# A block of attention and spectral filtering: projection loads in smaller parts, some of its products ahead of time, and the second norm taken from the spectrum

## The chip, the cores and the metric

One core of a Trainium2 chip runs the whole program. The metric is the device time of one execution in microseconds (us); the kernel before took 3833.35 us (median of three runs, 3829.59 to 3835.82). A profiled execution beside them gives the trace that is quoted below. Its engines are TensorE (PE; its weight loads are listed apart as PEld), VectorE (DVE), ScalarE (ACT), GpSimd (POOL) and SyncE (SP), which issues all DMA transfers of this kernel.

## What is computed

The input x has 2 images of 48 x 48 tokens with 768 channels, all in float32. Cut to what matters:

```python
x = x + attention(group_norm(x))     # 12 heads of 64, relative positions, a projection 768 x 768
x = x + spectral(group_norm(x))

def spectral(x):                     # x: 2, 48, 48, 768
    xf = rfft2(x, axes=(1, 2), norm="ortho")         # 48 x 25 frequencies
    o1 = gelu(block_matmul(xf, w1) + b1)             # 8 blocks of 96 channels, complex
    o2 = softshrink(block_matmul(o1, w2) + b2, 0.01) # 8 blocks of 96 channels, complex
    return irfft2(o2, s=(48, 48), norm="ortho")

def group_norm(v):                   # 32 groups of 24 channels, over all tokens of an image
    return (v - mean(v)) / sqrt(var(v) + 1e-5)
```

The second norm has no scale of its own, so it commutes with the Fourier transform: the mean sits in one coefficient of each channel, the one of frequency zero, and the division by the deviation is a factor on each channel. By Parseval's theorem the sum of squares over the tokens is also the sum of squares over the spectrum.

## The kernel before

The two images run one after the other. Each passes through four stages.

**Attention.** After the first norm, 108 units (6 pairs of heads, 6 groups of 384 queries, 3 thirds of a group) run through a loop whose order is written out by hand: operations recorded through `InOrder` (L59, all of them shown as L67 in the profile) keep the program's order on their engine. For a unit, PE computes the scores (`ps_s`), DVE adds the relative positions that POOL has laid out (L342) and takes the maximum, ACT takes the exponential, DVE transposes squares of 32, and SP moves the pieces to their place in `pT`, six DMAs per half of a unit. Two turns later `weigh` multiplies `pT` by the values into `ps_o`, and `finish` stores the result, group by group, in the DRAM tensor `oT`; the softmax denominators go to `inv_d`, inverted, for half of a pair's groups at a time. In the last turns of the loop, L555 calls `late()` seven times; each call runs one step of the class `Projection` (L572), beside the attention's own work.

**Projection.** `Projection` owns one large SBUF tile: the weights `w` (6 blocks of 128 rows by 768), the bias `pb`, two buffers for `oT` and one for the inverses. Its seven steps (L586) load the weights in two halves, then nothing, then `tokens(0)`, nothing, the bias, and `values_bias`, which for the first image adds the values' bias multiplied by the projection's weights (`ps_pb`, 12 matmuls). `tokens(g)` (L625) loads 384 columns of `oT` in one DMA and the inverses in two, and POOL multiplies them (L639). `project_out` (L643) loads the residual x in six parts of 4 x 96 rows at its start, adds the bias on POOL (L657), and then runs over 18 tiles of 128 tokens. For each tile and each half of the channels PE makes a product `acc` of six matmuls (L693), and DVE adds it into x in pieces whose rows stay inside one of the 96-row parts (`shifts`, L702). Behind the products, `over_w` (L665) transforms two image rows at a time along w: four matmuls `ps_y`, four ACT copies, and one DMA to the DRAM tensor `y_d`. `tile_stats` (L723) takes the sum and the squared deviations of each 96-row part on DVE, POOL and ACT for the second norm; `join_stats` (L736) joins them after the last tile, with two matmuls `js_tot` and a square root on ACT.

**Spectrum.** `Spectral.run` (L998) goes over 8 blocks of 96 channels, two of which make a slab. `load` reads a slab's `y_d` into five `y2` tiles (L867). `over_h` (L870) transforms along h: 25 small matmuls in five groups `ps_z`, which DVE and ACT in turn copy to the one buffer `z`. `scale` multiplies the weights w1 by the deviation's inverse, and `constant` subtracts the mean from the frequency zero. `first` (L893) is the product with w1, 24 records of 400 columns for PE and a GELU on ACT; `second` (L914) is the product with w2, where DVE adds the bias (L939) and clips (L945) and POOL subtracts (L946). In `run`, block n goes through `over_h(n)`, `second(n-1)`, `first(n)`, in this order on PE. `back_h` and `back_w` return to image rows, through the DRAM tensor `u_d`, and write `out`.

What is not recorded through `InOrder` is placed by a scheduler when the program is built: in this kernel the products, the x loads and additions, the stats and most of the spectrum. All of it shares one pool of seven PSUM banks (`ps_b`); `ps_o` has a bank to itself.

Of the kernel before, what the change touches and what calls it, by code (L numbers as in the profile page):

```python
# [9 lines left out]
F32 = mybir.dt.float32  # L10
AF = mybir.ActivationFunctionType
ALU = mybir.AluOpType
# [4 lines left out]
P = 128  # L17
# [144 lines left out]
def attention(tc, k, x_b, a, oT, inv_d, late, span, ps_b, ps_o):  # L162

# [10 lines left out]
    with ExitStack() as ctx:  # L174
# [319 lines left out]
        for n in range(len(order) + 3):  # L494
# [33 lines left out]
            if turn is not None:  # L528
                turn()
                turn = None  # L530
            if n > 1 and recent:
                older = recent.pop(0)
                weigh(older)
# [38 lines left out]
class Projection:  # L572


    def __init__(self, tc, k, a, oT, inv_d, span, ps_b, dram):
# [7 lines left out]
        self.o = {}  # L583
        w_v = a["proj_w"].rearrange("(cc p) f -> p cc f", p=P)
        half = NCC // 2
        self.steps = [  # L586
            lambda: nc.sync.dma_start(out=self.w[:, :half], in_=w_v[:, :half]),
            lambda: nc.sync.dma_start(out=self.w[:, half:], in_=w_v[:, half:]),
            lambda: None,
            lambda: self.tokens(0),  # L590
            lambda: None,
            self.bias,
            self.values_bias,
        ]

    def step(self):
        self.steps.pop(0)()

# [5 lines left out]
    def values_bias(self):  # L604


        nc, k = self.nc, self.k
        if k.pb_d is not None:
            return
        for hf in range(2):  # L610
            cols = slice(hf * UQ, (hf + 1) * UQ)
            ps = self.ps_b.tile([P, 512], F32, tag="b", name="ps_pb")
            for cc in range(NCC):
                nc.tensor.matmul(
                    ps[:, :UQ],
                    lhsT=k.bv[:, cc : cc + 1].to_broadcast([P, P]),
                    rhs=self.w[:, cc, cols],
                    start=(cc == 0),
                    stop=(cc == NCC - 1),
                )  # L620
            nc.vector.tensor_tensor(self.pb[:, cols], ps[:, :UQ], self.pb[:, cols], ALU.add)
        k.pb_d = self.dram.tile([C], F32, tag="pb_d", name="pb_d")
        nc.sync.dma_start(out=k.pb_d, in_=self.pb[0, :])

    def tokens(self, g):  # L625

        nc = self.nc
# [5 lines left out]
        nc.sync.dma_start(out=o_sb, in_=self.oT_v[:, :, g * UQ : (g + 1) * UQ])  # L633
        for h in range(2):
            nc.sync.dma_start(
# [3 lines left out]
        nc.gpsimd.tensor_tensor(o_sb, o_sb, inv, ALU.mult)  # L639
        self.o[g] = o_sb  # L640


def project_out(tc, k, x_b, pr, pools, y_d, x2, stats, constants):  # L643
# [6 lines left out]
    ps_b, small, work = pools  # L650
# [3 lines left out]
    for i, part in enumerate(x2):  # L654
        nc.sync.dma_start(out=part, in_=x_v[:, i * XP : (i + 1) * XP, :])
        for j in range(XP):
            nc.gpsimd.tensor_tensor(part[:, j, :], part[:, j, :], pr.pb[:R], ALU.add)  # L657
        if i == 0:
            constants()
            pr.tokens(1)  # L660
    row = lambda hp: x2[hp // XP][:, hp % XP, :]
    local = small.tile([R, HW // 2, NG], F32, tag="local", name="local")
    dev = small.tile([R, HW // 2, NG], F32, tag="dev", name="dev")

    def over_w(g):  # L665
# [4 lines left out]
        for s in range(C // SC):  # L670
# [10 lines left out]
        nc.sync.dma_start(out=y_d[:, 2 * g : 2 * g + 2, :], in_=y1)  # L681

    done = turned = 0
    for t in range(NT):
        if t % 3 == 0:
            if t // 3 not in pr.o:
                pr.tokens(t // 3)
            o_sb = pr.o[t // 3]
        for hf in range(2):
            cols = slice(hf * UQ, (hf + 1) * UQ)  # L690
            acc = bank("acc")
            for cc in range(NCC):
                nc.tensor.matmul(  # L693
                    acc[:, :UQ],
                    lhsT=o_sb[:, cc, (t % 3) * P : (t % 3 + 1) * P],
                    rhs=pr.w[:, cc, cols],
                    start=(cc == 0),
                    stop=(cc == NCC - 1),
                )
# [3 lines left out]
        while (turned + 1) * 2 * R <= (t - 1) * P:  # L703
            over_w(turned)
            turned += 1
        while (done + 1) * R <= (t + 1) * P:
            tile_stats(
                nc,
                lambda name: work.tile([R, C], F32, tag="st", name=name),
                row(done),  # L710
                local[:, done, :],
                dev[:, done, :],
            )
            done += 1
    while turned < HW // 4:
        over_w(turned)
        turned += 1
    mean, rstd = join_stats(nc, k, small, bank, local, dev)
    nc.vector.tensor_copy(stats[:, 0, :], mean)
    nc.vector.tensor_copy(stats[:, 1, :], rstd)  # L720


def tile_stats(nc, work, xt, local, dev):  # L723

    x3 = xt.rearrange("p (g d) -> p g d", d=GC)
    nc.vector.tensor_reduce(local, x3, AX.X, ALU.add)
    nc.vector.tensor_scalar(local, local, 1.0 / GC, None, ALU.mult)  # L727
    xc = work("st_xc").rearrange("p (g d) -> p g d", d=GC)
    nc.gpsimd.tensor_tensor(  # L729
        xc, x3, local[:, :, None].to_broadcast([xt.shape[0], NG, GC]), ALU.subtract  # L730
    )
    nc.scalar.activation(xc, xc, AF.Square)  # L732
# [447 lines left out]
```

## Time and profile before

| what | us |
|---|---|
| median of three runs | 3833.35 |
| the profiled execution's own time | 3833.92 |
| its span, first to last instruction | 3831.8 |
| image 0: first product to last ps_y on PE | 1471.29 to 1660.7 |
| image 0: spectrum, first ps_z to last ps_x | 1672.05 to 1912.8 |
| image 1: first product to last ps_y on PE | 3382.52 to 3572.1 |
| image 1: first ps_z | 3583.56 |
| L693 products, PE busy, both images | 293.7 |
| L729 POOL / L732 ACT, busy, both images | 70.9 / 40.5 |

The mean clock granted to PE over the span is 0.978 of full speed. A row of the page's fifth part gives the line, engine, operation, output and input tile with their shapes, the count, then the busy time and the mean of one in ns, and then how long the engine was idle just before and who ended that. Matmuls in float32 appear as two records each, so the 12 matmuls of one tile's products are 24 records. The timeline lists the same instructions in order of time, neighbours of a kind merged. A row of the windows gives, for a stretch of time, the busy time of PE, PEld, DVE, ACT and POOL, the clock granted to PE, and the busy share and rate of the DMA engines.

### The profile page before, as it was taken

The page shows a single profiled execution, that of the slowest core. Times are in us where ns is not written, and L with a number is a line of the kernel's source. Part 1 is how long each engine was busy: PE and PEld are TensorE (multiplying, and loading weights), DVE is VectorE, ACT ScalarE, POOL GpSimd, SP SyncE. Part 2 cuts the span into 40 slices and gives each one's busy share as a digit, 9 for nine tenths or more (in the row PEclk, how much of TensorE's full clock was granted, in tenths as well). Part 3 has the DMA queues.
Part 4 walks back from the last instruction along what each step waited for, and adds up shares of the span by engine and source line. Part 5 has one row for each costly group of instructions (what it writes and reads, how often), then busy time and mean ns, then how long its engine had stood idle before and what let it go on. Part 6 is the DMA issues. An engine that isn't in the chain of part 4 may idle for free.

```text
span 3831.8 us, 83222 instructions
## 1 busy us (share of the span) xinstructions
PE 3657.1 (95%) x31464; PEld 2591.2 (68%) x31464; DVE 2940.4 (77%) x6642; ACT 2501.8 (65%) x3550; POOL 2063.8 (54%) x646
## 2 busy tenths in 40 slices
PE   8999999999999888989989999999999999779899
PEld 6677777767777655566666767777677776555665
DVE  5788888989889884654557988988888889846544
ACT  3788888888888882222137888888888888822221
POOL 2566666666666666422125666666666666663121
PEclk9999999999999999999999999999999999989899
DMA  3677777777777888434526787777777777884344
GB/s 109 144 175 170 169 175 167 177 160 175 169 171 170 172 194 199 128 85 125 175 74 143 171 176 169 172 171 173 167 175 167 173 169 164 203 192 124 88 122 134
DMA packets 496092, 606.92 MB, mean 158 GB/s; under 512 B 180109, under 2 KB 310797, under 8 KB 495694
## 3 DMA queue, kind: packets, MB, share of 16 engines
q1 hardware_dynamic: 495694, 601.61, 67.3%
q8 instruction: 250, 4.10, 0.5%
q14 instruction: 148, 1.21, 0.1%
HBM read 131.53 MB, written 87.67 MB: 57 GB/s over the span
## 4 chain that ended last, share of the span: by engine, by line
PE 80%; DMA 7%; DVE 4%; POOL 4%; SPq 3%; issue 1%; ACT 1%; POOLq 0%; DVEq 0%
PE ps_o L67 20%; PE ps_s L67 19%; PE ps_proj L67 14%; PE ps_v L67 8%; PE acc L693 5%; PE ps L929 4%; DVE s L67 3%; POOL s L342 3%; DMA pT<-s 3%; SPq L67 2%; PE ps_z L877 2%; PE ps_u L960 2%; PE ps L902 2%; PE ps L906 2%; PE ps_r L67 2%; DMA x<-in_x 1%
## 5 line engine op out<-in xcount | busy, mean ns | idle before, releaser
L342 POOL TENSOR_TENSOR s<-rhw 128x2304 f32<-128x2304 f32 x432 | 1744.7, 4060 | 1144.6 <-DMA pT<-s 596.9
L67 DVE CUSTOM_DVE_ANT_0 s<-ps_s,s 128x512 f32<-128x512 f32 (+1 forms) x2160 | 1224.0, 633 | 373.7 <-issue 248.3
L67 ACT ACTIVATE s<-s,nm 128x1152 f32<-128x1152 f32 x864 | 1074.7, 1245 | 451.7 <-DVE nm L67 414.1
L67 DVE STREAM_TRANSPOSE s<-s 128x1152 f32<-128x1152 f32 x864 | 1111.8, 1344 | 5.5 <-ACT s L67 5.5
L67 ACT COPY pT<-s 32x1152 f32<-32x1152 f32 x864 | 993.3, 1150 | 24.6 <-PE ps_o L67 9.2
L67 PE MATMUL ps_o<-pT,v 128*64 128x128 f32 x15552 | 923.9, 279 | 75.2 <-DMA pT<-s 47.4
L67 PEld LDWEIGHTS ps_o<-pT,v 128*64 128x64 f32 x15552 | 872.2, 140 | 138.2 <-issue 61.6
L67 PE MATMUL ps_s<-kT,qT 64*128 64x512 f32 (+1 forms) x4320 | 919.5, 558 | 13.8 <-DVE mx L67 9.9
L67 PEld LDWEIGHTS ps_s<-kT,qT 64*128 64x128 f32 x4320 | 431.0, 186 | 452.3 <-issue 334.8
L67 PE MATMUL ps_proj<-xnT,w 128*128 128x384 f32 (+1 forms) x2016 | 597.3, 450 | 2.3 <-ACT gn_rstd L150 2.3
L67 PEld LDWEIGHTS ps_proj<-xnT,w 128*128 128x128 f32 x2016 | 360.5, 191 | 209.6 <-DVE mx L67 41.1
L693 PE MATMUL acc<-proj 128*128 128x384 f32 x864 | 293.7, 500 | 21.4 <-DVE x L702 11.9
L67 PEld LDWEIGHTS ps_v<-w,xnT 128*128 128x128 f32 x2592 | 295.8, 193 | 21.2 <-DVE mx L67 21.2
L67 PE MATMUL ps_v<-w,xnT 128*128 128x128 f32 x2592 | 308.0, 278 | 0.0
L946 POOL TENSOR_TENSOR spectrum<-spectrum 128x480 f32<-128x480 f32 x80 | 96.3, 1203 | 324.9 <-DVE spectrum L945 322.0
L693 PEld LDWEIGHTS acc<-proj 128*128 128x128 f32 x864 | 168.9, 196 | 142.6 <-issue 22.9
L732 ACT ACTIVATE st_xc<-st_xc 96x768 f32<-96x768 f32 x48 | 40.5, 843 | 233.8 <-POOL st_xc L729 233.8
L67 DVE DVE_READ_ACCUMULATOR2_ANT mx<- 128x1 f32 x2160 | 179.8, 83 | 0.0
L702 DVE TENSOR_TENSOR x<-acc,x 32x384 f32<-32x384 f32 (+2 forms) x216 | 119.6, 554 | 78.4 <-PE acc L693 74.4
L67 ACT ACTIVATION_READ_ACCUMULATOR s<-s,nm 128x1 f32 x864 | 161.1, 186 | 0.0
L729 POOL TENSOR_TENSOR st_xc<-x,local 96x768 f32<-96x768 f32 x48 | 70.9, 1481 | 145.6 <-DVE local L727 129.0
L910 ACT ACTIVATE spectrum<-ps,b 96x400 f32<-96x400 f32 x96 | 56.6, 590 | 138.7 <-PE ps L906 138.7
(96 smaller groups left out, 2194.7 us busy)
## 6 DMA issues: line engine op xcount, KB each, us to landing
pT<-s SPq DMA_DIRECT2D x2592, 144.0 KB
t<-rel SPq DMA_DIRECT2D x144, 189.0 KB
rhw<-t SPq DMA_DIRECT2D x144, 144.0 KB
y_d<-y SPq DMA_DIRECT2D x24, 672.0 KB
y<-y_d SPq DMA_DIRECT2D x40, 360.0 KB
u_d<-spectrum SPq DMA_DIRECT2D x40, 360.0 KB
u<-u_d SPq DMA_DIRECT2D x48, 300.0 KB
xt<-in_x SPq DMA_DIRECT2D x12, 1152.0 KB
```

Of the source, the lines that this page charges most:

```text
L67: return lambda *args, **kw: self.tc.keep_in_program_order(op(*args, **kw))
L342: nc.gpsimd.tensor_tensor(s[:, h, :].rearrange("p (y x) -> p y x", x=HW), rhw[:, x, h, :HW][:, :, None].to_broadcast([P, HW, HW]), rhw[:, ...
L693: nc.tensor.matmul(acc[:, :UQ], lhsT=o_sb[:, cc, (t % 3) * P : (t % 3 + 1) * P], rhs=pr.w[:, cc, cols], start=(cc == 0), stop=(cc == NCC - 1),
L702: nc.vector.tensor_tensor(dst, acc[p : p + n, :UQ], dst, ALU.add)
L729: nc.gpsimd.tensor_tensor(xc, x3, local[:, :, None].to_broadcast([xt.shape[0], NG, GC]), ALU.subtract)
L877: nc.tensor.matmul(ps[:BS, w * 96 : (w + 1) * 96], lhsT=self.y2[s, j][:, w, i * BS : (i + 1) * BS], rhs=k.fh, start=True, stop=True,)
L902: nc.tensor.matmul(ps[:BS, :400], lhsT=w1[:, wa, i, :], rhs=zf[:, 0, fs], start=True, stop=False,)
L906: nc.tensor.matmul(ps[:BS, :400], lhsT=w1[:, wb, i, :], rhs=zf[:, 1, fs], start=False, stop=True,)
L910: nc.scalar.activation(self.o1[:, ri, fs], ps[:BS, :400], AF.Gelu, bias=self.b1[:, n, ri : ri + 1])
L929: nc.tensor.matmul(ps[64 * r : 64 * r + 64, w * BS : (w + 1) * BS], lhsT=self.o1[:, ri, f0 : f0 + 64], rhs=w2[:, (0, 2, 1, 0)[2 * r + ri], ...
L946: nc.gpsimd.tensor_tensor(val, val, clip, ALU.subtract)
L960: nc.tensor.matmul(ps[: 2 * HW, :480], lhsT=k.ih, rhs=d2[:, c0 : c0 + 480], start=True, stop=True)
```

## The change

The change has four parts.

1. `tile_stats`, `join_stats`, `norm`, `scale` and `constant` go. In `Spectral`, each block's squares are summed on ACT as soon as its groups are in `z` (`square`: twice for the frequencies that stand for two, once for the first and last column), `mean(n)` subtracts the group's mean from the frequency zero after a matmul with the constant matrix `gmean` (one column, `ps_nm`), and `norm(n)` joins the sums over a group with a second such matmul (`ps_nv`), takes the inverse square root on DVE by a shift of the bits and three Newton steps, and scales block n's part of w1.
2. `z` has two buffers, and `over_h(n+1)` runs ahead of `second(n-1)` and `first(n)`. The mean and the norm of block n+1 stand inside `second(n-1)`, after its first and fourth group.
3. `Projection` loads its weights in six parts over three turns, `oT` in two halves, and issues its loads, multiplications and products in program order (`InOrder`, so these show as L68). `tokens(1)` is a step of its own in the last turns. `fill` puts matmuls between the last three `weigh` calls: for image 0 one half of `values_bias`, then the other and one product, then three products; for image 1 none, two and three products. The loads of `tokens(g+1)` and of part g+1 of x are issued at the start of group g, instead of as early as the scheduler places them.
4. The last two `over_w` run in two halves of the channels, each behind the last tile's product of that half, and each half has a DMA to `y_d` of its own.

On PE the last turns of image 0 are then: scores of the last unit, ps_pb, ps_o, ps_pb, one product, ps_o, three products, ps_o, and the remaining products with ps_y between them. On SP the inverses of `tokens(0)` are issued one before and one after the twelve pT transfers of the last turn with scores, and `tokens(1)` after the last six.

```diff
+            if n >= len(order) - 1 and recent:
+                late(n - len(order) + 2)
             if n > 1 and recent:
                 older = recent.pop(0)
                 weigh(older)
...
         self.steps = [
-            lambda: nc.sync.dma_start(out=self.w[:, :half], in_=w_v[:, :half]),
-            lambda: nc.sync.dma_start(out=self.w[:, half:], in_=w_v[:, half:]),
-            lambda: None,
-            lambda: self.tokens(0),
-            lambda: None,
-            self.bias,
-            self.values_bias,
+            lambda: (load(0), load(1)),
+            lambda: (load(2), load(3)),
+            lambda: (load(4), load(5)),
+            lambda: (next(parts), self.bias()),
+            lambda: next(parts),
+            lambda: list(parts),
+            lambda: self.tokens(1),
         ]
+        self.accs, self.waiting, self.late = {}, [], 1
+        if k.pb_d is None:
+            self.late = 0
+            self.waiting += [lambda hf=hf: self.values_bias(hf) for hf in range(2)]
+        for t in range(3):
+            self.waiting += [lambda t=t, hf=hf: self.product(t, hf) for hf in range(2)]
...
+    def fill(self, n):
+        for _ in range(n - self.late):
+            self.waiting.pop(0)()
+        self.late = 0
...
+    def parts(self, g):
...
+        for h in range(2):
+            cc = slice(h * NCC // 2, (h + 1) * NCC // 2)
+            self.sync.dma_start(out=o_sb[:, cc], in_=self.oT_v[:, cc, g * UQ : (g + 1) * UQ])
+            if h == 0:
+                yield
         for h in range(2):
-            nc.sync.dma_start(
+            self.sync.dma_start(
                 out=inv[h * HD : (h + 1) * HD],
                 in_=self.inv_d[:, g // 3, h, g % 3, :].partition_broadcast(HD),
             )
-        nc.gpsimd.tensor_tensor(o_sb, o_sb, inv, ALU.mult)
+            if h == 0:
+                yield
+        self.pool.tensor_tensor(o_sb, o_sb, inv, ALU.mult)
...
     for t in range(NT):
-        if t % 3 == 0:
-            if t // 3 not in pr.o:
-                pr.tokens(t // 3)
-            o_sb = pr.o[t // 3]
+        if t % 3 == 0 and 0 < t < NT - 3:
+            pr.tokens(t // 3 + 1)
+            rows(t // 3 + 1)
         for hf in range(2):
             cols = slice(hf * UQ, (hf + 1) * UQ)
-            acc = bank("acc")
...
+            acc = pr.product(t, hf)
             for p, hp, q, n in shifts(t):
                 dst = row(hp)[q : q + n, cols]
                 nc.vector.tensor_tensor(dst, acc[p : p + n, :UQ], dst, ALU.add)
+            if t == NT - 1:
+                half = C // SC // 2
+                for g in range(turned, HW // 4):
+                    over_w(g, range(hf * half, (hf + 1) * half))
...
+    def square(self, part, total):
+        r, w, h = part.shape[1:]
+        junk = self.junk[:, : r * w * h].rearrange("p (r w h) -> p r w h", r=r, h=h)
+        self.nc.scalar.activation(junk, part, AF.Square, accum_out=total)
...
+    def mean(self, n):
+        nc, z = self.nc, self.z[n % 2]
+        z0 = z[:, 0, 0, 0:1]
+        mean = self.bank("ps_nm")
+        nc.tensor.matmul(mean[:BS, :1], lhsT=self.k.gmean, rhs=z0, start=True, stop=True)
+        nc.vector.tensor_tensor(z0, z0, mean[:BS, :1], ALU.subtract)
+        self.square(z[:, :, :: KW - 1, :], self.power[n][:, KW // WP :])
+
+    def norm(self, n):
...
+        ps = self.bank("ps_nv")
+        nc.tensor.matmul(ps[:BS, :1], lhsT=self.k.gmean, rhs=total, start=True, stop=True)
+        nc.vector.tensor_scalar(var, ps[:BS, :1], 1.0 / S, GN_EPS, ALU.mult, ALU.add)
+        bits = rstd.bitcast(I32)
+        nc.vector.tensor_scalar(bits, var.bitcast(I32), 1, None, ALU.arith_shift_right)
+        nc.vector.tensor_scalar(bits, bits, -1, 0x5F3759DF, ALU.mult, ALU.add)
+        for _ in range(3):
+            nc.vector.tensor_scalar(fit, rstd, rstd, var, ALU.mult, ALU.mult)
+            nc.vector.tensor_scalar(fit, fit, -0.5, 1.5, ALU.mult, ALU.add)
+            nc.vector.tensor_tensor(rstd, rstd, fit, ALU.mult)
         w = self.w[s][0]
...
+        nc.vector.tensor_scalar(w[:, :, i, :], w[:, :, i, :], rstd, None, ALU.mult)
...
+        over_h(0)
         for n in range(NBK + 1):
...
+            if ahead:
+                over_h(ahead)
             if n:
-                self.second(n - 1)
+                self.second(n - 1, ahead)
+            else:
+                self.mean(ahead)
             if n < NBK:
                 self.first(n)
...
+            if n == 0:
+                self.norm(ahead)
+            elif i == 0:
                 self.back_w(s - 2, True)
```

## Prediction

> **What bounds the kernel now.** I read the page first: TensorE (PE) is busy 95% of the span, and the attention loop, which the change leaves alone, is most of it. An average says nothing about the stages that change, so I took PE's timeline where each image passes from attention to projection to spectrum (image 0; columns: start us, length us, engine, line, operation, count, and in brackets the idle time before and who ended it).
>
> ```profile
> PE 3657.1 (95%) x31464; PEld 2591.2 (68%) x31464; DVE 2940.4 (77%) x6642; ACT 2501.8 (65%) x3550; POOL 2063.8 (54%) x646
> ...
> 1438.15 8.01 PE L614 MATMUL ps_pb<-proj,bv 128*128 128x384 f32 x24
> 1447.46 4.15 PE L67 MATMUL ps_o<-pT,v 128*64 128x128 f32 x72 [1.30 <-DMA pT<-s]
> 1454.99 5.82 PE L67 MATMUL ps_o<-pT,v 128*64 128x128 f32 x72 [3.38 <-DMA pT<-s]
> 1465.43 5.81 PE L67 MATMUL ps_o<-pT,v 128*64 128x128 f32 x72 [4.63 <-DMA pT<-s]
> ...
> 1471.29 31.13 PE L693 MATMUL acc<-proj 128*128 128x384 f32 x96
> ...
> 1527.68 7.11 PE L693 MATMUL acc<-proj 128*128 128x384 f32 x12 [8.48 <-DVE x L702]
> 1539.66 10.13 PE L693 MATMUL acc<-proj 128*128 128x384 f32 x24 [4.87 <-POOL proj L639]
> ...
> 1655.43 5.33 PE L673 MATMUL ps_y<-x,fw 96*112 96x384 f32 x16
> 1661.53 0.41 PE L743 MATMUL js_tot<-js_part,ones 96*128 96x32 f32 x2 [0.77 <-DVE js_part L741]
> 1669.49 0.60 PE L756 MATMUL js_tot<-js_part,ones 96*128 96x32 f32 x2 [7.56 <-DVE dc L815]
> 1672.05 7.15 PE L877 MATMUL ps_z<-fh,y 96*96 96x96 f32 x50 [1.95 <-DMA y<-y_d]
> ...
> 1690.00:1740.00 50.00, 50.00 (x565) 35.75 (x564) 20.49 (x34) 12.48 (x22) 12.73 (x12) 1.00 0.37 95
> ```
>
> The reader is to see four regimes. (1) The last three ps_o wait for pT transfers; the windows give DMA shares of 0.86 to 1.07 there, so the rings are full. (2) In the projection PE is full except for two holes. After each it also runs slowly: 12 records take 7.11 us where 24 take 7.74 elsewhere, and 24 take 10.13. So the holes cost 8.48+4.87 plus about 3.2+2.4, or 19 us. In image 1 the holes are 3.35, 3.39 and 4.67, with 3.3+2.5 behind them: 17. (3) From the last ps_y (E = 1660.7) to the first spectral product (1679.04) PE does 4.25 us of work in 18.3. The waits name the norm's matmul, but the chain ends on a transfer: y_d is written from 1664.16 to 1668, y read until 1678.07. (4) In the spectrum PE is busy 50.00 of 50.00 us, DVE 20.5, ACT 12.5: only added PE work or a new PE wait costs there.
>
> **Part 1, stats removed.** 24 x L729 POOL (1.48), L732 ACT (0.84), L726/L727/L733 DVE (0.94, 0.18, 0.95) per image and the js chain go. Nothing of it is PE work; its worth is in the holes: L702, which frees PE's banks, stood behind L733 on DVE, which waited for ACT, which waited for POOL, where L729 stood behind whole blocks of x additions. **Gain 19 and 17 us, if the new order has no holes of its own.** Loads of group g+1 are now issued after group g-1's products. Two token loads (2.36 MB) and x (1.18 MB) at the 230 GB/s of the windows take 15 us, POOL 5.06+7.1 more; PE spends 6x3.87+2x2.58 = 28.4 us on a group, so the scaled tokens (some 18 us after issue, POOL's x work following them) are early by 10 us, and seven banks cover x. SP issues in order: it stands at the last oT and inv_d writes until ps_o ends, before tokens(2), which are not needed for another 30 us; y_d queued behind needs no haste until the end.
>
> **Part 2, products ahead.** Image 0 puts 4 products, image 1 puts 5, of 3.87 us into the holes of regime 1. Beside each stands its queue: PE keeps its order, so ps_o of the last-but-one unit stands behind product (0,0), which needs POOL's L639 over the whole of o_sb. The last quarter of what that waits for, inv of the second half, is issued after the last-but-one twelve pT: where before has the bias.
>
> ```profile
> 1447.18 9.14 SPq L67 DMA_DIRECT2D pT<-s  x12
> 1456.37 0.59 SPq L602 DMA_DIRECT2D proj<-in_proj_b  x1
> 1457.06 3.79 SPq L67 DMA_DIRECT2D pT<-s  x6
> ```
>
> That bias (384 KB) released DVE at 1461.07, 4.7 us after issue; inv has 576 KB, so about 1462, plus 5.06 on POOL: product (0,0) starts near 1467. Then PE: 3.87 (+3.2 slow after 11 us of idling), ps_o 4.15, three products 11.6, ps_o 4.15: 1494, with 15.5 us of products done. Before stood at 1471.2 with none, so the early products do not gain but **lose 1494-15.5-1471.2 = 7 us**. Image 1 likewise: inv issued near 3366, product at 3376.5, 7.74+3.2+4.15+11.6+4.15 gives 3407.4 with 19.4 done, against 3382.4: **lose 5.6**. I take 7 and 6. If inv needs only its own 2.7 us at 216 GB/s they are 4 and 3; if seven pieces of 144 KB must pass first (4.8 us more), 9 and 8. Two ps_pb in two parts: same work. The first half's addition of the bias (0.55) now stands before DVE's last transposes; SP is full of pT until 1456 anyway.
>
> A rule speaks against this part: the Trainium skill, "DMA: Bandwidth & Descriptors", section "Rules for kernel authors", wants 1 MiB per DMA[...]. The row first: pT pieces of 144 KB hold 203 to 216 GB/s from 1440 to 1470. The change makes weights of 384 KB and tokens of 576 KB: 4+6 more transfers per image. By the rule's page ("Anatomy of one DMA", about 2 us fixed, measured there on another issue path) that is 20 us an image if each stood alone; by the row, nothing but about 0.5 us of SP each, since the ring is full. I take the row.
>
> **Part 3, the end of the projection.** The last half's y goes out in two channel halves. The last product half (3.87) and two pairs of ps_y with L702's 4x0.55 before the second pair (about 1.1 us of waiting each, **2.2 lost**) then follow the first half's write. It is issued at about E-6.9 instead of E+3.5; with the same 7.9 us of write and read (1664.16 to 1672.05) ps_z starts at E+1, paced by five reads at 1.5, done E+8. The second block's 4.25 us follow (E+12.3).
>
> Now the norm is late next. Block 0's last square on ACT ends near E+9, ps_nm and a square of the DC column E+10.7, ps_nv E+11.3, then 11 dependent DVE operations. Nearest rows, each 0.18 long and 0.22 apart:
>
> ```profile
> 1670.84 0.18 DVE L720 COPY stats<-js_rstd 128x32 f32<-128x32 f32 x1
> 1671.06 0.19 DVE L804 TENSOR_TENSOR pick<-stats,gmask 96x32 f32<-96x32 f32 x1
> 1671.28 0.18 DVE L811 TENSOR_REDUCE col<-pick 96x8 f32<-96x32 f32 x1
> ```
>
> 2.6 us with the mean of block 1 between, 0.4 for L869: first(0) at E+15. Before: E+18.3 with block 1's 4.25 still to do. **Gain 18.3+4.25-15 = 7.5 per image** (2 if PE starts cold, as image 1 did: 9.8 us for 8.06; 11 if the DVE chain hides).
>
> **Part 4, the spectrum.** Per image 16 matmuls of one column are added, 12 of them outside the gap above. The row: gn_mean (L131, two columns) takes 2.02 us for 14 records, 7 matmuls, so 0.29 each: **3.5 us lost**. The skill's "TensorE: Matmul & The Clock Gate", section "Wait — 56ns, not 53.3ns?", has a floor of 25 ns per start: at two records each that would be 0.6 us. A single js_tot took 0.41: 5 us. I take the row. ACT adds six squares a block: 768 wide is 0.84 (L732), so 0.55 to 0.6 at 480 with its accumulation read; with two or three copies at 0.56 they end about 1.5 us after the block's transform. ps_nv is 6.7 us after it: no wait. On DVE the chain (nine operations, 2 us) precedes the last L958; before, L946 ended 0.45 us ahead of its ps_u, so four blocks lose about 0.4: **1.6**. The second z buffer and over_h ahead gain nothing where PE is full. The next image's first xt loads go earlier: they are hidden either way. Sqrt's table load goes (1.28, ACT, idle anyway).
>
> **Sum.** Image 0: 19-7-2.2+7.5-5.1 = 12.2; image 1: 17-6-2.2+7.5-5.1 = 11.2. Together 23.4. The profiled execution took 3833.92 (span 3831.8 plus 2), the median of the three is 3833.35: 3833.4-23.4 = **3810 us**. Own range 3798 to 3822, from the ends of parts 2 to 4.
>
> **Rivals.** *A, the tail also hides its products*: inv lands early since less is queued ahead, part 2 gains 2 to 4 us per image instead of losing, and the transition reaches 11: 3833-2x(18+3-2+11-4) = 3781 to 3790. For it: tokens no longer stand before twenty-four pT. Against: the bytes ahead of the last pT are the same. *B, slower*: PE's order makes the tail decide. Product (0,0) holds two ps_o, so bank, oT, the inverses and all later token loads follow it. Each us that inv or POOL is later costs one per image; from 12 us beyond my 1467 (1479) the gain is gone, and at 1485, with the second group's loads then also late (SP stands behind oT), it is 3833+2x6 = 3845. For it: 8 outstanding pieces at a DMA share near 1; against: the bias's 4.7 us. *C, the holes refill*: the projection's loads, issued a group at a time, leave some 10 us of holes of their own (POOL waits for tokens while the DMA also carries x); the stats were the name on the wait only: 3831. Against: 10 us of slack in part 1.
>
> **Chances.** Main 0.55, A 0.20, B 0.15, C 0.10. The measurement can tell about 0.2% (7.7 us) from no change. Faster 0.75, same 0.10, slower 0.15. Leaving out half of B and the far end of A: 3784 to 3835.
>
> **What would show it.** Right: no DVE or POOL wait of PE between the seventh product and E; products (0,0) preceded by some 10 us idle on POOL L68 proj; first(0) some 15 us after E; ps_nm and ps_nv near 0.29 and PE busy 50 of 50 in mid-spectrum. Wrong: holes before group 2 or 3, PE waits at ps_nv, or the last ps_o much past 1500.

## The result and the profile after

Four executions of the changed kernel took 3808.99 to 3818.63 us, median **3812.08**; beside them the kernel before took 3832.66. The ratio is 0.9942, 95% interval 0.9930 to 0.9955: 20.6 us faster, where 23.4 were forecast. The profiled execution is the longest of the four (3818.63, span 3816.8), so it shows only 15.0 us of gain against the profiled execution of before.

The first row of the page, PE's timeline where image 0 leaves attention, and the rows of SP and POOL that belong to product (0,0):

```profile
PE 3660.0 (96%) x31520; PEld 2596.1 (68%) x31520; DVE 2845.0 (75%) x6692; ACT 2516.4 (66%) x3690; POOL 1993.1 (52%) x598
```
```profile
1440.04 4.14 PE L68 MATMUL ps_pb<-proj,bv 128*128 128x384 f32 x12
1444.10 4.15 PE L68 MATMUL ps_o<-pT,v 128*64 128x128 f32 x72
1448.18 4.14 PE L68 MATMUL ps_pb<-proj,bv 128*128 128x384 f32 x12
1470.60 6.50 PE L68 MATMUL acc<-proj 128*128 128x384 f32 x12 [18.28 <-POOL proj L68]
1477.03 4.15 PE L68 MATMUL ps_o<-pT,v 128*64 128x128 f32 x72
1481.11 11.88 PE L68 MATMUL acc<-proj 128*128 128x384 f32 x36
1492.92 4.15 PE L68 MATMUL ps_o<-pT,v 128*64 128x128 f32 x72
```
```profile
1457.26 0.62 SPq L68 DMA_DIRECT2D proj<-inv_d  x1
```
```profile
1465.51 5.03 POOL L68 TENSOR_TENSOR proj<-proj 128x2304 f32<-128x2304 f32 x1 [27.88 <-DMA pT<-s]
```

Read them from the bottom. POOL starts 8.25 us after SP has issued the last quarter of what it waits for, the inverses' second half; product (0,0) follows POOL's 5 us; and both remaining ps_o stand behind product (0,0). (POOL's row names a pT transfer as the last that it waited for; in image 1 its row names the inverses, and POOL starts 6.30 us after their issue.) Ahead of product (0,0) PE idles 18.28 us, and the twelve records then take 6.50 instead of 3.87. In image 1 the same wait is 22.20.

The passage from projection to spectrum, image 0, in PE's timeline of the changed kernel, and a row of the windows from mid-spectrum:

```profile
1653.35 1.52 PE L721 MATMUL ps_y<-x,fw 96*112 96x384 f32 x4 [1.15 <-DVE x L742]
1654.70 1.86 PE L892 MATMUL ps_z<-fh,y 96*96 96x96 f32 x20
1657.28 1.06 PE L892 MATMUL ps_z<-fh,y 96*96 96x96 f32 x10 [0.72 <-DMA y<-y_d]
1660.95 6.24 PE L892 MATMUL ps_z<-fh,y 96*96 96x96 f32 x40 [2.62 <-DMA y<-y_d]
1667.03 0.25 PE L842 MATMUL ps_nm<-spectrum,gmean 96*96 96x1 f32 x2
...
1668.89 0.25 PE L858 MATMUL ps_nv<-nm_total,gmean 96*96 96x1 f32 x2
...
1673.01 1.27 PE L920 MATMUL ps<-spectrum,w 96*96 96x400 f32 x2 [2.84 <-issue]
```
```profile
1690.00:1740.00 50.00, 50.00 (x548) 35.70 (x544) 25.00 (x59) 18.93 (x44) 12.72 (x12) 1.00 0.42 116
```

SP's rows of the same stretch, with the reads of y (`y<-y_d`) among the writes (`y_d<-y`):

```profile
1650.37 0.84 SPq L878 DMA_DIRECT2D y<-y_d  x2
1652.74 0.30 SPq L68 DMA_DIRECT2D y_d<-y  x1
1653.09 0.46 SPq L878 DMA_DIRECT2D y<-y_d  x1
1655.40 0.30 SPq L68 DMA_DIRECT2D y_d<-y  x1
1655.75 14.66 SPq L878 DMA_DIRECT2D y<-y_d  x10
```

And, from the kernel before, the transform of a block that no wait precedes:

```profile
1687.10 4.41 PE L877 MATMUL ps_z<-fh,y 96*96 96x96 f32 x50
```

The first ps_z waits for nothing now (E, the end of the last ps_y, is 1654.87), but the third and fourth pieces of y are late, 40 records behind that wait take 6.24 us instead of 3.5 (by the last row's rate), and first(0) is at E+18.1. In mid-spectrum PE is still busy 50.00 of 50.00.

To see where the time went I cut each image into three stretches that do not overlap. **Tail**: from the end of the last score product to the start of ps_i (the end of the last ps_o), less 3.87 us for each product already done. **Body**: from there to E, the end of the last ps_y, plus those products. **Rest**: from E to the next image's first transposition, or to the end of the span.

| us, image 0 / image 1 | tail | body | rest |
|---|---|---|---|
| before | 33.0 / 33.3 | 189.6 / 189.7 | 252.1 / 259.7 |
| changed | 41.4 / 38.7 | 173.3 / 173.3 | 253.8 / 263.2 |
| gain | -8.4 / -5.4 | +16.3 / +16.4 | -1.7 / -3.5 |

That sums to 13.7; what stands ahead of the tails gives the other 1.3 (image 0's attention ends 1.9 later, image 1's takes 3.8 less, its first norm 0.5 more). Almost all of the gain is in the body. The tail loses, as forecast, and the rest, which was to gain 2.4 per image, loses.

### The profile page after: what moved, and what is told of

It is laid out like the page before. It is cut to its first block, busy times and chain, and to the rows that moved or that the text cites. A ratio compares the mean times of both kernels' runs of the same rounds, so it can differ in the third digit from the quotient of the medians.

```text
span 3816.8 us, 83418 instructions
## 1 busy us (share of the span) xinstructions
PE 3660.0 (96%) x31520; PEld 2596.1 (68%) x31520; DVE 2845.0 (75%) x6692; ACT 2516.4 (66%) x3690; POOL 1993.1 (52%) x598
## 4 chain that ended last, share of the span: by engine, by line
PE 84%; DMA 5%; DVE 4%; POOL 3%; SPq 2%; issue 1%; ACT 1%; POOLq 0%; DVEq 0%; ACTq 0%
PE ps_o L68 20%; PE ps_s L68 19%; PE ps_proj L68 14%; PE ps_v L68 8%; PE acc L68 7%; PE ps L948 4%; DVE s L68 3%; POOL s L344 3%; DMA pT<-s 2%; PE ps_z L892 2%; PE ps L920 2%; PE ps L924 2%; PE ps_u L983 2%; SPq L68 2%; PE ps_y L721 2%; PE ps_r L68 1%
## 5 line engine op out<-in xcount | busy, mean ns | idle before, releaser
L68 DVE CUSTOM_DVE_ANT_0 s<-ps_s,s 128x512 f32<-128x512 f32 (+1 forms) x2160 | 1223.6, 633 | 371.7 <-issue 243.3
L68 ACT ACTIVATE s<-s,nm 128x1152 f32<-128x1152 f32 x864 | 1074.7, 1245 | 452.5 <-DVE nm L68 414.8
L68 DVE STREAM_TRANSPOSE s<-s 128x1152 f32<-128x1152 f32 x864 | 1111.8, 1344 | 5.5 <-ACT s L68 5.5
L68 ACT COPY pT<-s 32x1152 f32<-32x1152 f32 x864 | 993.2, 1150 | 19.5 <-DVE s L68 2.1
L68 PE MATMUL ps_o<-pT,v 128*64 128x128 f32 x15552 | 919.7, 278 | 47.9 <-DMA pT<-s 21.8
L68 PEld LDWEIGHTS ps_o<-pT,v 128*64 128x64 f32 x15552 | 867.8, 140 | 112.2 <-issue 53.8
L68 PE MATMUL ps_s<-kT,qT 64*128 64x512 f32 (+1 forms) x4320 | 918.5, 558 | 13.4 <-DVE mx L68 9.8
L68 PEld LDWEIGHTS ps_s<-kT,qT 64*128 64x128 f32 x4320 | 431.4, 186 | 450.7 <-issue 333.9
L68 PE MATMUL ps_proj<-xnT,w 128*128 128x384 f32 (+1 forms) x2016 | 597.0, 450 | 2.3 <-ACT gn_rstd L151 2.3
L68 PEld LDWEIGHTS ps_proj<-xnT,w 128*128 128x128 f32 x2016 | 360.8, 191 | 209.0 <-DVE mx L68 41.0
L68 PE MATMUL acc<-proj 128*128 128x384 f32 x864 | 287.5, 492 | 40.5 <-POOL proj L68 40.5
L68 PEld LDWEIGHTS ps_v<-w,xnT 128*128 128x128 f32 x2592 | 295.9, 193 | 21.2 <-DVE mx L68 21.2
L68 PE MATMUL ps_v<-w,xnT 128*128 128x128 f32 x2592 | 308.1, 279 | 0.0
L68 PEld LDWEIGHTS acc<-proj 128*128 128x128 f32 x864 | 165.8, 193 | 156.6 <-POOL proj L68 41.3
L728 ACT COPY y<-ps_y 112x384 f32<-112x384 f32 x96 | 45.9, 478 | 265.8 <-PE ps_y L721 248.7
L68 DVE DVE_READ_ACCUMULATOR2_ANT mx<- 128x1 f32 x2160 | 178.9, 83 | 0.0
L68 POOL TENSOR_TENSOR proj<-proj 128x2304 f32<-128x2304 f32 x12 | 60.6, 5052 | 197.5 <-DMA proj<-inv_d 169.7
L68 ACT ACTIVATION_READ_ACCUMULATOR s<-s,nm 128x1 f32 x864 | 161.1, 186 | 0.0
```

Of the source, the lines that this page charges most:

```text
L68: return lambda *args, **kw: self.tc.keep_in_program_order(op(*args, **kw))
L728: nc.scalar.copy(y1[:, :, ch], ps[:YP, : 2 * SC].rearrange("p (t c) -> p t c", c=SC))
```

## The experiments

Each run has runs of the kernel before beside it (median 3833.97, 3836.40 or 3831.31 us), so runs are compared by their ratio to those; 0.001 is 3.8 us. The changed kernel has 0.9942. Each ratio is known to about 0.0014 either way, so two ratios that differ by less than about 0.002 are not told apart by the times. The differences in tail, body and rest come from one profiled execution of each kernel. The diffs are cut, and are against the changed kernel where nothing else is said.

### Are the early products worth their place?

The changed kernel without products between the weighings:

```diff
-        for t in range(3):
-            self.waiting += [lambda t=t, hf=hf: self.product(t, hf) for hf in range(2)]
...
-        for _ in range(n - self.late):
+        for _ in range(min(n - self.late, len(self.waiting), 1)):
```

> The changed kernel without the products that it places between the last weighings (the two halves of the value bias stay where they are); everything else as changed. Theory: those products lose time because the first of them holds two ps_o behind POOL's L68, so without them the last ps_o ends near 1475 us in image 0 instead of 1497, and though 15.5 us of products (19.4 in image 1) are then still to do, the time falls by the 7 and 6 us of the prediction, perhaps 8 to 10: 3794 to 3800 us against 3812. Rival A (the tail hides its products): they are worth 2 to 4 us per image, and the time rises to 3816 to 3820. Rival: the last ps_o is set by the pT transfers and not by PE's order: then all 35 us of products come on top and the time is 3840 or more.

Measured: 3803.82 us, ratio 0.9921 (0.9908 to 0.9935), 8 us below the changed kernel: on the theory's side, though short of its range. The last two weighings of image 0 wait for pT again, as before the change:

```profile
1453.46 6.45 PE L68 MATMUL ps_o<-pT,v 128*64 128x128 f32 x72 [4.42 <-DMA pT<-s]
1464.67 5.82 PE L68 MATMUL ps_o<-pT,v 128*64 128x128 f32 x72 [4.76 <-DMA pT<-s]
```

The last one ends at 1470.5 instead of 1497.1. The tail returns to 33.6 / 34.8, the body stays at 173.3 / 173.3. The products lose, by 7.8 and 3.9 us of tail. Rival A is out, and so is the rival by which the tail is set by transfers alone: the early products filled no time, since PE idled for longer ahead of them.

### What holds them up?

First the tokens of group 0, one turn earlier:

```diff
-            lambda: (load(0), load(1)),
-            lambda: (load(2), load(3)),
-            lambda: (load(4), load(5)),
+            lambda: (load(0), load(1), load(2)),
+            lambda: (load(3), load(4), load(5)),
             lambda: (next(parts), self.bias()),
             lambda: next(parts),
             lambda: list(parts),
+            lambda: None,
             lambda: self.tokens(1),
```

> The changed kernel with the loads of the first token group one turn earlier (weights in two steps instead of three, the second half of inv before the last twenty-four pT), early products kept. Theory: the 18.3 and 22.2 us that PE waits on POOL before product (0,0) come from the place of that load in SP's order; POOL's product should start near 1450 us, product (0,0) follow the ps_pb or ps_o in front of it with at most a few us of waiting, and the last ps_o end near 1475 to 1480 with 15.5 us of products done: 17 to 22 us less per image, 3768 to 3778 us. Rival: the ring is full, the bytes brought forward delay the pT transfers by as much, and the weighings wait instead: 3795 to 3812 us.

Measured: 3812.52 us, ratio 0.9932 (0.9919 to 0.9945): a miss in the time, though the wait went as expected. PE's timeline of this kernel, two rows of SP's and one of POOL's, which adds the bias to x:

```profile
1453.72 7.13 PE L68 MATMUL acc<-proj 128*128 128x384 f32 x12 [3.73 <-POOL proj L68]
...
1480.87 11.78 PE L68 MATMUL acc<-proj 128*128 128x384 f32 x36
1496.07 5.83 PE L68 MATMUL acc<-proj 128*128 128x384 f32 x12 [3.42 <-DVE x L742]
```
```profile
1481.16 0.34 SPq L68 DMA_DIRECT2D oT<-res  x1
...
1484.02 0.45 SPq L68 DMA_DIRECT2D x<-in_x  x1
```
```profile
1491.87 8.85 POOL L68 TENSOR_TENSOR x<-x,proj 96x768 f32<-96x768 f32 x5 [15.35 <-DMA x<-in_x]
```

The wait of 18.28 is 3.73 (in image 1 that of 22.20 is 5.59), and the tail is 27.5 / 26.4, 12 to 14 us shorter. But after seven products PE stops: all seven banks hold products that DVE cannot add, because x is not there. In this build SP has x's load behind the last oT write, and so behind the last ps_o, which three products keep waiting; the changed kernel has the load at 1471.91, ahead of that write. The body is 5.4 and 8.8 us longer (in image 1 the wait on DVE is 7.03). A wait was removed, and another took more than half of its gain: 14.2 of 26.2 us in the traces. Their difference flatters this kernel, since its profiled execution is the shortest of five and the changed kernel's the longest of four; the ratios do not tell the two kernels apart.

So the next run, on top of this one, leaves the three products of the last turn behind the last weighing:

```diff
-        for _ in range(n - self.late):
+        for _ in range(n - self.late if n < 3 else 0):
```

> The kernel with the first token group a turn earlier, and of the early products only those in the gap before the last-but-one weighing (one in image 0, two in image 1); the three before the last weighing go behind it. Theory: in the run with the earlier tokens PE no longer waited 18 and 22 us for POOL, but SP, which has x's loads behind the last oT write, got them out only at 1484 us, so that seven banks filled and PE waited 3.4 and 7.0 us for DVE L742. With the last ps_o 12 us earlier, x is loaded 12 us earlier and these two waits and their slow records go: 12 to 15 us less than with all products early, 3795 to 3800 us. Rival: the waits on L742 come from DVE's own backlog and stay: 3809 to 3813 us.

Measured: 3793.87 us, ratio 0.9889 (0.9876 to 0.9903): 20 us below the changed kernel and just below the theory's range. Its PE timeline:

```profile
1455.33 5.83 PE L68 MATMUL acc<-proj 128*128 128x384 f32 x12 [3.63 <-POOL proj L68]
1461.09 4.15 PE L68 MATMUL ps_o<-pT,v 128*64 128x128 f32 x72
1465.60 4.15 PE L68 MATMUL ps_o<-pT,v 128*64 128x128 f32 x72 [0.36 <-ACT res L68]
...
1469.80 27.26 PE L68 MATMUL acc<-proj 128*128 128x384 f32 x84
```

The last ps_o ends 27 us earlier than in the changed kernel, with one product done ahead instead of four; the tail is 26.3 / 28.3, the body again 173.3. The waits on DVE are gone, so they were the order of x's load on SP's queue, not DVE's backlog. Against the kernel without early products it is some 12 us faster by the ratio, and three products (one, and two in image 1) are 11.6; no run has the earlier loads without any product ahead, so how the 12 us divide between the two is not shown.

One turn further back, against that run:

```diff
-            lambda: (next(parts), self.bias()),
-            lambda: next(parts),
-            lambda: list(parts),
+            lambda: (next(parts), next(parts)),
+            lambda: (list(parts), self.bias()),
+            lambda: None,
             lambda: None,
```

> The kernel of 3793.9 us with the first token group's loads one turn earlier still (both oT halves and the first inv in the third step, the second inv and the bias in the fourth). Theory: PE's remaining waits on POOL before product (0,0), 3.6 us in image 0 and 6.8 in image 1, with some 2 and 2.8 us of slow records behind them, are still the place of inv in SP's order; they fall to those of the pT transfers, and the time to 3783 to 3789 us. Rival: the transfers brought forward delay the twenty-four pT behind them, and earlier weighings wait by as much: 3791 to 3798 us.

Measured: 3792.62 us, ratio 0.9893 (0.9878 to 0.9908), no change: the rival's time, a miss of the theory. PE no longer waits for POOL (tail 24.7 / 20.4), but ps_o waits for pT earlier: from image 1's first product with qkv_w to its last score product it is 1408.2 us, against 1403.0 in the run before, and image 0's last score product ends 5.3 us later. Transfers brought forward here delay others by about as much.

### The price of a transfer

The kernel of 3793.87 us with larger transfers, ten fewer per image:

```diff
-        load = lambda cc: nc.sync.dma_start(out=self.w[:, cc], in_=w_v[:, cc])
+        load = lambda cc: nc.sync.dma_start(out=self.w[:, cc : cc + 3], in_=w_v[:, cc : cc + 3])
...
-        for h in range(2):
-            cc = slice(h * NCC // 2, (h + 1) * NCC // 2)
-            self.sync.dma_start(out=o_sb[:, cc], in_=self.oT_v[:, cc, g * UQ : (g + 1) * UQ])
-            if h == 0:
-                yield
+        self.sync.dma_start(out=o_sb, in_=self.oT_v[:, :, g * UQ : (g + 1) * UQ])
+        yield
```

> The earlier tokens with the products before the last-but-one weighing only (3793.9 us as measured), but its weights loaded in two transfers of 1.18 MB as before the change instead of six of 0.39 MB, and each group's oT in one of 1.18 MB instead of two of 0.59: ten transfers less per image, and nothing else. It weighs the two prices of the prediction's split. Rule (about 2 us fixed per transfer): 20 us per image are saved if each stood alone, 3754 us; some 3774 if half of it shows. Row (the ring is full, a transfer costs SP some 0.5 us): 3790 to 3797 us. Below nothing: the last quarter of what POOL waits for is not changed, so a loss could only come from an oT load that is waited for whole; up to 2 us.

Measured: 3790.19 us, ratio 0.9883 (0.9866 to 0.9900), against 0.9889: the row, not the rule. What the large transfers change is where the time goes: image 1's attention is 1407.0 us to its last score product instead of 1403.0, and the tail 24.3 instead of 28.3. The kernel before and the one of the next section, which also load pieces of 1.18 MB, have 1406.5 and 1406.6 us there; the other kernels with small pieces, save that of the run above, have 1402.1 to 1405.0. That fits a pT transfer that waits longer behind 1.18 MB, which no row here shows by itself; the four microseconds come back in the tail. It would also account for the 3.8 us by which image 1's attention is shorter in the changed kernel.

### Statistics or order?

The spectrum's norm as changed, but `Projection` and `project_out` as before the change, only without `tile_stats` and `join_stats` (the lines are against the kernel before):

```diff
-        while (done + 1) * R <= (t + 1) * P:
-            tile_stats(
...
-            done += 1
-    mean, rstd = join_stats(nc, k, small, bank, local, dev)
```

> The statistics removed and the spectrum's norm as changed, but the projection with the loads, the step list and the place of every load as before the change: whole halves of the weights, tokens(0) in one step, all x rows up front, no products ahead, y whole. It asks which of the two closes the projection's holes. Theory: the holes that end on DVE L702 (8.48 and 3.2 slow in image 0; 3.35, 3.39 and 3.3 slow in image 1) go with the statistics; those that end on POOL L639 (4.87+2.4; 4.67+2.5) stand behind x rows of later groups and stay. Then, with the spectrum's loss of some 4.5 us an image and a transition some 1 us better or worse than before: 3833.5-11.7-10+9 = 3821 us, 2 to 3 us each way. Rival (the statistics were all of it): both kinds go, 3806 us. Rival (they were only the name on the wait): both stay, 3843 us.

Measured: 3825.06 us, ratio 0.9969 (0.9958 to 0.9980): by the ratio 12 us below the kernel before, as the theory has it. One hole is left in its PE timeline (in image 1 one of 6.06):

```profile
1534.38 10.40 PE L693 MATMUL acc<-proj 128*128 128x384 f32 x24 [6.71 <-POOL proj L641]
```

The waits on DVE are gone, the one on POOL stays. The body is 180.0 / 179.5: the statistics cost 9.6 and 10.2 us of it, and the order of the loads the rest.

### The end of the projection

The last rows written whole, as before:

```diff
-            if t == NT - 1:
-                half = C // SC // 2
-                for g in range(turned, HW // 4):
-                    over_w(g, range(hf * half, (hf + 1) * half))
+        if t == NT - 1:
+            for g in range(turned, HW // 4):
+                over_w(g)
```

> The changed kernel with the last rows' transforms over w written whole, after the last product, as before the change. Theory: the early half write is worth some 6 to 8 us per image less the 2.2 us of its two waits; E is 2 us earlier, the first ps_z waits for y some 8 us after E, and first(0) starts near E+23: 3820 to 3826 us. Rival: the transition is set by the reads of y and the norm's chain of small operations, not by when y is written, and the time stays 3810 to 3814.

Measured: 3819.53 us, ratio 0.9955 (0.9943 to 0.9968), 5 us above the changed kernel: on the theory's side, short of its range, and not clear of the noise of two ratios. The body is 170.6 / 170.6 without the waits of the halves, 2.7 less; the first ps_z waits 8.0 us for y, and first(0) is at E+23.3 / E+23.5. So the halves are worth some 2.5 us per image by the time, not 6 to 8, and not certainly anything: from E to block 0's second product the traces have 38.6 and 37.8 us, against 32.5 and 37.0 in the changed kernel.

What then holds first(0)? The first block's norm, moved ahead of the second block's transform:

```diff
-            if n == 1 and j == 1:
-                self.mean(0)
-            if n == 1 and j == 3:
-                self.norm(0)
+            if n == 1 and j == 1:
+                self.norm(0)
...
             self.square(z[:, :, w0:w1, :], self.power[n][:, j : j + 1])
+        if n == 0:
+            self.mean(0)
```

> The changed kernel with the first block's ps_nm right behind its own ps_z (not behind two pieces of the second block), and its ps_nv after two pieces instead of four. Theory: first(0), at E+18.1 and E+21.1 us, waits for a chain that begins at ps_nm, which PE reaches only after 20 records of the second block at a low clock: the chain starts 2 to 3 us earlier, and so does first(0): 3806 to 3808 us against 3812. Rival: the second block's transforms and the reads of y set it, so that the chain's time is only moved: 3811 to 3813 us.

Measured: 3812.79 us, ratio 0.9940 (0.9927 to 0.9954): no change, and a miss. First(0) is not even earlier (E+19.8 / E+20.3): the second block's records, still at the low clock, now run behind ps_nv instead of ahead of it, and first(0) stands behind them. From E to the second product of block 0 it is 32.5 us in image 0, exactly as in the changed kernel. A small gain can't be excluded: with this order the stretch takes 32.5 to 32.9 us in all four cases (two images here, two in the next run), with the changed kernel's order 32.5 to 37.5 us in the twelve of six kernels. Two microseconds per image are less than the times can show.

Both together, the earlier tokens (with the one product, two in image 1, of the 3793.87 us kernel) and the earlier norm:

> The earlier tokens with only the products before the last-but-one weighing, and the earlier ps_nm and ps_nv of the first block, together. Theory: the two gains add: 3789 to 3796 us, faster than the changed kernel by 0.4 to 0.6%. Rival: one of them is taken back by the other's neighbour (the x rows or the y reads): 3797 to 3808 us.

Measured: 3793.55 us, ratio 0.9883 (0.9868 to 0.9898). That is inside the theory's range, but the earlier tokens alone have 0.9889, so no second gain is shown.

The last run adds to this kernel five products that nobody reads, where PE waits for y:

```diff
         for j in range(KW // WP):
+            spare = (0, 0, 1, 4, 0)[j] if n == 0 else 0
+            if spare:
+                idle = self.bank("ps_idle")
+            for _ in range(spare):
+                nc.tensor.matmul(
+                    idle[:YP, : 2 * SC], lhsT=k.fw, rhs=self.x2[0][:, 0:2, :SC],
+                    start=True, stop=True,
+                )
             ps = self.bank("ps_z")
```

> The kernel with both changes (3793.6 us), with one and four products of 0.65 us, whose result nobody reads, put on PE where it waits 0.8 and 2.3 to 2.7 us for the reads of y behind the last ps_y. Theory: the 70 to 90 spectral records behind these waits run at half speed (20 in 3.5 us, 1.8 elsewhere) because PE idled before them; with PE busy they run in half the time, and the second spectral product of block 0 comes 4 to 6 us earlier: 3782 to 3786 us. Rival: the low speed is not made by these short waits, or the reads of y are then late by as much: 3791 to 3797 us, or 2 us above 3793.6 if the added products last longer than the waits.

Measured: 3784.36 us, ratio 0.9872 (0.9857 to 0.9886) against 0.9883. By the intervals alone that is not shown to be faster than the run before; the traces show the mechanism. The windows from E to first(0), first without and then with the idle products (after PE, PEld, DVE, ACT and POOL come the clock, the DMA share and the GB/s):

```profile
1637.50:1658.00 20.50, 15.76 (x108) 14.88 (x107) 6.21 (x22) 9.48 (x27) 0.00 (x0) 0.67 0.77 200
```
```profile
1644.00:1661.00 17.00, 13.34 (x118) 10.82 (x116) 6.08 (x22) 9.32 (x26) 0.00 (x0) 1.00 0.87 233
```

Ten records more, and PE is busy 2.4 us less, at a granted clock of 1.00 instead of 0.67. The same 20 records of ps_z, behind ps_nm, without and with:

```profile
1647.44 3.49 PE L892 MATMUL ps_z<-fh,y 96*96 96x96 f32 x20
```
```profile
1654.26 1.92 PE L900 MATMUL ps_z<-fh,y 96*96 96x96 f32 x20
```

From E to block 0's second product it is 29.3 / 27.8 us instead of 32.7 / 32.7. This version has the lowest ratio of all: 1.3% below the kernel before, 0.7% below the changed one.

### The price of a one-column product

```diff
-        nc.tensor.matmul(mean[:BS, :1], lhsT=self.k.gmean, rhs=z0, start=True, stop=True)
+        for _ in range(2):
+            nc.tensor.matmul(
+                mean[:BS, :1], lhsT=self.k.gmean, rhs=z0, start=True, stop=True
+            )
...
```

(and the same for ps_nv)

> The changed kernel with each one-column product of the norm (ps_nm, ps_nv) issued twice: 16 more per image, 12 of them where PE is full. Theory: each displaces 0.26 to 0.29 us, so 3.1 to 4.6 us more per image: 3818 to 3821 us. Rival (a start costs 25 ns): 0.4 to 0.8 us per image, 3812 to 3814 us. In the trace the time between the ps_1 or ps_2 groups on both sides of a doubled ps_nm should be 0.5 us or 0.05 us longer than without it.

Measured: 3821.34 us, ratio 0.9959 (0.9947 to 0.9972): 6.5 us above the changed kernel, 3.3 per image, just inside the noise of two ratios. The trace is the better measure. In the timeline of this kernel:

```profile
1707.95 0.50 PE L843 MATMUL ps_nm<-z,gmean 96*96 96x1 f32 x4
1708.38 3.52 PE L954 MATMUL ps<-w,spectrum 96*64 96x96 f32 x80
```

The next products start 0.43 us after the pair; after the single ps_nm of the changed kernel they start 0.26 us later (1710.83 to 1711.09). So the first costs 0.26 and a repetition with the same weights 0.17; the floor of 25 ns per start that the prediction weighed would have made the repetition, two records, 0.05.

## Why the prediction was right, and where it was off

The time (3810 against 3812) and the main case were right; its terms did not all have the right size.

- **Part 1, holes.** Right, in place and nearly in size. With the waits of the halves the body was to gain 16.8 and 14.8; it gained 16.3 and 16.4, and no DVE or POOL wait stands between the seventh product and the last tile. The split is near the one of the holes in its lines, 11.7 and 10.0 us behind DVE, 7.3 and 7.2 behind POOL: statistics some 10 us, order of the loads some 9 (180.0 / 179.5 to 170.6 / 170.6).
- **Part 2, products ahead.** Right in sign, mechanism and sum: the tails lose 8.4 and 5.4, 13.8 where 13 were forecast (11.9 with what stands ahead of them, back to the kernel's start or to image 1's first product with qkv_w: 10.3 and 1.6). What was short is the time from inv's issue to POOL: 8.25 us in image 0 and 6.30 in image 1, not 5.7. It varies: in the kernels with the same order of loads it is 6.0 to 8.5, and why is not shown. With an issue 0.9 later it put image 0's product (0,0) at 1470.6 instead of 1467. PE's idle time ahead of that product, some 10 us by the prediction's sign of being right, is 18.28 and 22.20. The uneven split between the images is inside what the attention itself varies: image 0's last score product ends between 1436.4 and 1444.8 us over the kernels here.
- **The split of transfers.** The row's price held; ten transfers more or less per image change nothing in the time that can be measured.
- **Part 3, the transition.** This term was mis-sized, and is the error of the sum: "first(0) at E+15", "**Gain 18.3+4.25-15 = 7.5 per image**". It was at E+18.1 and E+21.1. To the second product of block 0, which has one more block's transform (4.4 us) ahead of it than before, the gain is 2.6 and 1.3. The prediction let ps_z be paced by five reads at full clock. In the trace SP issues the third read of y, and all later ones, between and behind the second halves' writes (1653.09 and 1655.75, after 1650.37 for the first two), so PE waits 0.72 and 2.62 us, and the next records run at half speed: ps_nm is at E+12.2 instead of just before E+10.7, ps_nv at E+14.0 instead of E+11.3. Idle products bring first(0) from E+20.1 and E+20.0, in the kernel that they were added to, to E+16.7 and E+15.2, so the clock is 3 to 5 us of the miss; that is shown. That SP's order makes the reads late is read from the trace, and was not tried. The prediction gave a cold start its own price, a gain of 2, and did not take it. Its own row of before spoke for that price: the 50 records behind that wait took 7.15 us, which it counted as 4.25 us of work, the next 50 took 4.41.
- **Part 4, the spectrum.** 5.1 us forecast, 4.3 and 4.7 measured from block 0's second product to the end (the one block's transform of 4.4 us that now stands ahead of it set aside); PE has no wait at ps_nv in mid-spectrum. The row was the right choice over the floor.

The profiled execution accounts for 8.4 us less gain than forecast: 10.0 from parts 3 and 4, a first norm 0.5 longer, less some 1.1 in the tail and 1.1 in the body. Over four executions the median lies 6.5 us lower than this one, and no trace shows where those took less, so the close agreement of 3810 and 3812 is in part luck: of the mechanism, some 5 to 6 us per image in the transition were not foreseen. Of the rivals, A (the tail hides its products) fell by the run without them, C (holes refill) by the body. B's mechanism, PE's order in the tail deciding, is what happens; only its point of no gain, product (0,0) at 1479, was not reached at 1470.6. A's formula as it is written gives 3781; its upper end of 3790 does not come out of it.

## What to carry to other kernels

Work put ahead of a wait is free only if its own input is there before the wait begins; on an engine that keeps its order it otherwise lengthens the wait, and the check is when the last transfer it needs is issued, not how long the hole is. Here one turn earlier for that load, and fewer products in front of the last weighing, were worth as much again as the whole change. After removing a wait, look at what the same queue issues next: the load of x, held behind a write that the filler delayed, took more than half of the first attempt's gain.

## What was not expected of the hardware

- **The clock falls after short waits.** The Trainium skill, "TensorE: Matmul & The Clock Gate", section "Why this matters for your kernels", advises to avoid gaps of more than some 3 us. Here, from E on, waits of 0.77 and 2.29 us with 1 us of work between them (0.72 and 2.62 in the changed kernel) were followed by half speed: 20 records took 3.49 us, and 1.92 when the waits were filled, at a granted clock of 0.67 and 1.00 over the whole stretch. The measurement decides: in this place several shorter gaps close together were enough.
- **A one-column product is not nearly free.** It displaces 0.26 us with its weights new and 0.17 with the same weights, at 96 x 96 in float32 with two records each.
- **Large transfers among small ones shifted time here, and did not cost it.** With weights and oT in pieces of 1.18 MB image 1's attention is 4 us longer, and the tail 4 us shorter.
